# A two-layer image kernel: a gate's loads and the y stores issued in the middle of a tick instead of at its end

## The chip, the cores and the metric

The kernel runs on one core of a Trainium2 chip. The metric is the device time of one execution in microseconds; lower is better. Everything is float32.

## The reference

Input and output are `x` of shape 8 x 8 x 512 x 512 (batch elements, channels, rows, columns). Two residual layers follow each other, each on a group-normed input:

```python
x = x + L0(gn(x))        # spectral: a few Fourier modes of every channel, mixed and sent back
x = x + L1(gn(x))        # below

def L1(x):
    grid = x
    for _ in range(15):                               # coupled map: 15 steps per channel
        mapped = 3.9 * grid * (1 - grid)
        grid = 0.85 * (0.7 * mapped + 0.3 * conv3x3(mapped, K_local)) + 0.15 * x
    cml = clip(grid, 1e-4, 1 - 1e-4)
    nca = sigmoid(conv1x1(relu(conv3x3(x, Wp)), Wu))  # 128 hidden channels
    gin = concat([x, cml, nca])
    g = sigmoid(conv1x1(relu(conv3x3(gin, Wg1)), Wg2))
    return g * cml + (1 - g) * nca
```

## The kernel before

Four kinds of work are woven together by hand, and the order of the source is kept on every engine and queue (`keep_order`).

- *Steps.* The coupled map of an element lies in SBUF in sets of slabs: a first phase of four sets (channels 0 to 3) and a second of four sets and a tail. One step of one set is 96 matmuls (`Slabs.convolve`, L535), a `max` and add on DVE (L548), a square on ACT (L554), and an exchange of edge rows by DMA (`renew`: L581 and L582 on POOL's queue, L591 on SP's; the tail's on L648, L652 and L657). When a set has made its 15 steps, `leave` clips it and puts off its stores to the plane `cml` in HBM (L611) by one tick.
- *Rounds.* `Hidden.round` makes the 3x3 convolution to 128 hidden channels for four rows at a time (L734) from `cols`, which `load` (L717) brings in; `point` (L761) makes the 1x1 convolution after it. Every fourth round a tile `y` is full; ACT makes its sigmoid (L773), and its `store` to the plane `nca` (L776) is put off by one tick. `e.rows` counts the rows of `nca` that are stored.
- *Gates.* A gate is 12 rows of the final formula, 43 of them for each element. `load` takes two tiles from the shared slots: `gin` (three loads at L796, 1,024 KB together: input of the 3x3 convolution) and `mix` (three at L801, 576 KB: the rows that are mixed). `conv` (L811) gives `gin` back, `point` (L828, L832, L834) follows, and `finish` (L839) and the store to `out` (L846) are made after the first step of the next tick, and give `mix` back. The gates of an element are made while the next element takes its steps; the last element's gates are left for the end.
- *Spectral layer.* The next element's 16 channel tiles `x` come in (L183), go through layer 0 and are stored to the plane `xn` (L424).

A *tick* (`work`) is three steps, then `transfers()`, up to three rounds, and the matmuls of gates, hidden point and spectral pieces. `transfers()` issues the x loads and the loads of the next phase (`dE`, `dO`, L506). The gates' loads come last, with `others.load(gates)`, and then `tick()` advances the clock `now` and issues everything that was put off until then. There are 45 ticks for each element, and a final *drain* without steps for the last element's gates, in which `others.lag` is 2 and the y stores are issued from POOL's queue instead of SP's. Where `gates` is 2 in a tick with steps, one gate is loaded after the first step.

SBUF has 19 slots of 8 KB per partition. `shared.most` is 4, 7 or 3 of them, by the place in the element (`SHARED`, `MORE`, `LEAST`), for gates and the next element's `x`; of these `kept` are held back for `x`. Free slots are handed out in the order in which they came free, so a load into one may have to wait for the last reader of what lay there.

Of the kernel before, what the change touches and what calls it, by code (L numbers as in the profile page):

```python
# [41 lines left out]
P = 128  # L42
C = 8
N = 512
# [68 lines left out]
def view(t, offset, dims):  # L113

    return bass.AP(tensor=t.tensor, offset=t.offset + offset, ap=[list(d) for d in dims])
# [3 lines left out]
def conv_layers(ctx: ExitStack, tc: tile.TileContext, a, out):  # L119
# [10 lines left out]
    class Slots:  # L130
# [4 lines left out]
        def __init__(self, most):  # L135
            self.most, self.held = most, {}
# [15 lines left out]
    sets, shared = Slots(SLOTS), Slots(SHARED)  # L152
# [7 lines left out]
    pairs = [pp.tile([P, 2, N], F32, name=f"pair{i}") for i in range(4)]  # L160


    put_off, now = [], [0]

    def later(ticks, work):
        put_off.append((now[0] + ticks, work))
# [8 lines left out]
    def load(name, shape):  # L175
        t = cp.tile(shape, F32, name=name)
        nc.scalar.dma_start(out=t, in_=a[name])
        return t
# [8 lines left out]


    dft_y = load("dft_y", [P, 2, 32])
    dft_x = load("dft_x", [P, 2, 2, 8])  # L190
    waves = load("waves", [16, 5])
# [475 lines left out]
    class Phase:  # L667
# [23 lines left out]
        def squares(self, n):  # L691
            while self.squared < len(self.sets) and sets.room():
                if not self.ready(self.squared, 0, n + TICK):
                    break
                self.sets[self.squared].square()
                self.squared += 1
# [9 lines left out]
    class Hidden:  # L706
# [50 lines left out]
        def point(self, hs, ps):  # L757

            for r, h in hs:
                for g in range(4):  # L760
                    nc.tensor.matmul(  # L761
                        ps[32 * g : 32 * g + 32], w_u[:, r % 4], h[:, g],
                        start=(r == hs[0][0]), stop=(r == hs[-1][0]),
                        tile_position=(0, 32 * g),
                    )
            if hs[0][0] % 4 == 0:
                self.y = wk.tile([P, N], F32, tag="y", name="y", bufs=2)
                nc.scalar.copy(self.y, ps)  # L768
            else:
                nc.vector.tensor_tensor(self.y, self.y, ps, ALU.add)  # L770
            if r % 4 == 3:
                y, r0 = self.y, 4 * (r - 3)
                nc.scalar.activation(y, y, AF.Sigmoid, bias=b_u)  # L773

                def store():
                    (nc.gpsimd if others.lag else nc.sync).dma_start(  # L776
                        out=view(self.e.nca, (1 + r0) * C * N, [[N, P], [1, N]]), in_=y
                    )
                    self.e.rows = r0 + 16

                later(1, store)

    class Gate:

# [4 lines left out]
        def load(self):  # L789

            r0, self.at = self.r0, now[0]
            self.gin = shared.take([P, 4, N], "gin")
            self.mix = shared.take([P, 4, N], "mix")
            for q, src in enumerate((self.e.xn, self.e.cml, self.e.nca)):
                at, rows = (0, 48, 88)[q], (6, 5, 5)[q]
                nc.sync.dma_start(  # L796
                    out=self.gin[at : at + rows * C],
                    in_=view(src, r0 * C * N, [[N, rows * C], [3 * C * N, 4], [1, N]]),
                )
            for q, src in enumerate((self.e.xn, self.e.cml, self.e.nca)):  # L800
                nc.sync.dma_start(  # L801
                    out=self.mix[: GR * C, q],
                    in_=view(src, (r0 + 1) * C * N, [[N, GR * C], [1, N]]),
                )

        def conv(self, ps):

            gin, (x1, d, ng) = self.gin, (self.mix[: GR * C, q] for q in range(3))
            for n, (dx, lo, hi, at) in enumerate(SHIFTS):
                for j in range(4):  # L810
                    nc.tensor.matmul(  # L811
                        ps[32 * j : 32 * j + 32, lo:hi], gband[:, dx], gin[:, j, at : at + hi - lo],
                        start=(n == 0), stop=(n == 2), tile_position=(0, 32 * j),
                    )

            nc.gpsimd.tensor_tensor(d, d, ng, ALU.subtract)  # L816
            nc.vector.scalar_tensor_tensor(  # L817
                x1, x1, self.e.back[: GR * C, 1:2], ng, ALU.mult, ALU.add
            )
            shared.drop(gin)  # L820
            nc.vector.tensor_scalar(self.mix[:, 3], ps, b_g1, 0.0, ALU.add, ALU.max)  # L821
# [92 lines left out]
    class Others:  # L914


        def __init__(self):
            self.before, self.after, self.hold, self.limit = None, None, 0, 0
            self.mapped, self.lag = deque(), 0
            self.loaded, self.convolved, self.pointed = deque(), deque(), deque()  # L920

        def load(self, limit):
            if self.mapped and not (self.before and self.busy()):
                self.before = self.mapped.popleft()
            e, after = self.before, self.after
            kept = max(0, after.most() - len(after.x)) if after and after.pieces else 0
            for _ in range(limit):
                if not (e and e.gates) or shared.room() - kept < 2:
                    break
                if e.rows < min(e.gates[0].r0 + GR + 1, N) or len(e.mapped) <= 2 * SETS:  # L930
                    break
                g = e.gates.popleft()
                g.load()
                self.loaded.append(g)

        def busy(self):
            return self.before.gates or self.loaded or self.convolved or self.pointed

        def finish(self):
            while self.pointed:  # L940
                self.pointed.popleft().finish()

        def conv(self, ps):
            if not self.loaded or now[0] < self.hold or self.loaded[0].at + self.lag > now[0]:
                return False
            g = self.loaded.popleft()
            g.conv(ps)
            self.convolved.append((g, ps))
            return True
# [42 lines left out]
    def element(b):  # L992
        e = Element(b)
        phase(e.halves[0])
        phase(e.halves[1] + [e.tail])
        elements.append(e)
        return e

    e = element(0)
# [3 lines left out]
    others = Others()  # L1003
    for n in count():
# [5 lines left out]
        ps = next(turns)  # L1010
# [15 lines left out]
    def work(steps, rounds, e, after, gates, transfers, squares=lambda: None):  # L1026

        def half():
            used[0] += 1
            return halves[used[0] % 2]  # L1030

        settled = iter(())
        for n, (s, step) in enumerate(steps):
            ps = half()
            s.convolve(step, ps)
            next(settled, None)
            settled = s.settle(step, ps)
            next(settled)
            others.finish()
            if gates == 2:  # L1040
                others.load(1)
                gates = 1
        others.finish()
        transfers()
        for _ in range(rounds):
            e.hidden.round(half(), after, settled)
        next(settled, None)
        squares()


        first, second = halves[used[0] % 2], halves[(used[0] + 1) % 2]
        if not others.spectral(WIDE, second):
            used[0] += 1
            first, second = second, first
        groups = e.hidden.sums()
        if len(groups) == 2:
            e.hidden.point(groups.pop(0), first[1][:, 0])
        others.conv(first[0][:, 0])
        others.spectral(EARLY, [second[0][:, 0]])
        two = others.conv(second[0][:, 0])  # L1060
        if groups:
            e.hidden.point(groups[0], first[1][:, 1])
        others.spectral(FILL, [None])
        others.spectral(LATE, [second[1][:, 0], second[0][:, 0]])
        others.point()
        used[0] += two
        others.load(gates)
        tick()
        squares()

    def turn(at, rounds, e, after, gates):


        now_phases = [p for p in phases if at < p.end + TICK]

        def transfers():
            if others.after:
                others.after.fetch()
            for p in now_phases:
                p.fetch(at)  # L1080

        def squares():
            for p in now_phases:
                p.squares(at)

        for p in now_phases:
            p.prepare(at)
        steps = [slots[i] for i in range(at, at + TICK) if 0 <= i < len(slots)]
        work(steps, rounds, e, after and after.hidden, gates, transfers, squares)
# [4 lines left out]
    for b in range(B):  # L1094
        e = elements[b]
# [3 lines left out]
        first, second = phases[2 * b : 2 * b + 2]  # L1099
# [14 lines left out]
        for t in range(ticks):  # L1114
# [8 lines left out]
            gates = open_[t] + (left > sum(open_[t:]) and not (after and after.pieces))  # L1123
# [68 lines left out]
```

## Time and profile before

| | us |
|---|---|
| median of 3 runs | 9339.16 |
| lowest and highest | 9327.55, 9340.95 |
| the profiled execution | 9328.59 |
| its span, first to last instruction | 9326.8 |
| PE busy | 8776.0 |
| DVE, ACT, POOL busy | 5685.6, 4101.0, 3378.9 |
| mean granted clock of PE | 0.987 |

A row of a group in the profile names the line of the kernel, the engine and the operation, what is written and read (buffer numbers left out), how many there were, the busy time and the mean of one in ns; after the second bar stands the engine's idle time just before these instructions, and what ended most of it. "issue" means that no other engine and no transfer in the profile ended the wait. A row of waits gives total us, times and longest. SPq is SP's DMA queue. A row of the timeline gives the start, the time taken, and the instructions of one kind that follow each other. A row of a table of windows has the stretch, its length, the busy time of PE, PEld, DVE, ACT and POOL with counts, the granted clock of PE, the busy share of the DMA engines and the GB/s they moved.

### The profile page before, as it was taken

How to read it: one execution, taken by the hardware profiler on the slowest of the kernel's cores; microseconds unless marked ns; L12 is line 12 of the kernel's file. 1: busy time of each engine (PE TensorE's matmuls, PEld its weight loads, DVE VectorE, ACT ScalarE, POOL GpSimd, SP SyncE). 2: the span in 40 equal slices, each digit the busy share in tenths (PEclk: the TensorE clock that was granted, in tenths of full speed). 3: DMA queues.
4: the chain of work that ended last, by engine and by line, in shares of the span. 5: the costliest groups of instructions: out<-in, count | busy, mean ns of one | idle time of the engine just before them, and what ended most of it. 6: DMA issues, size and time to landing. Idle time of an engine off the chain costs nothing. (4 is left out here: it accounts for less than half of the span.)

```text
span 9326.8 us, 334742 instructions
## 1 busy us (share of the span) xinstructions
PE 8776.0 (94%) x150992; PEld 4165.1 (45%) x150992; DVE 5685.6 (61%) x5844; ACT 4101.0 (44%) x4285; POOL 3378.9 (36%) x4441
## 2 busy tenths in 40 slices
PE   5999999999999999999999999999999999899988
PEld 2445544444444444444444444444444444344433
DVE  5665567556665567655676556755567555555655
ACT  2445444444444444444444444444444444344422
POOL 3242334334343243433334343343433324453422
PEclk9999999999999999999999999999999999999999
DMA  5241356745566455754657546575455755665487
GB/s 158 79 127 39 96 150 167 171 109 152 148 178 146 112 155 145 184 137 112 169 146 176 129 108 167 156 179 126 111 158 167 173 117 129 144 153 119 105 212 184
DMA packets 697414, 1327.26 MB, mean 142 GB/s; under 512 B 146939, under 2 KB 152443, under 8 KB 668499
## 3 DMA queue, kind: packets, MB, share of 16 engines
q1 hardware_dynamic: 591840, 1244.38, 51.8%
q0 software_dynamic: 101792, 60.33, 3.0%
q8 instruction: 1187, 19.45, 0.9%
q14 instruction: 241, 1.97, 0.1%
q10 hardware_dynamic: 2354, 1.14, 0.0%
HBM read 977.48 MB, written 270.61 MB: 134 GB/s over the span
## 5 line engine op out<-in xcount | busy, mean ns | idle before, releaser
L535 PE MATMUL pair<-m,band 32*32 32x512 f32 x103680 | 3669.8, 605 | 205.2 <-issue 132.7
L554 ACT ACTIVATE m<-m 128x1024 f32<-128x1024 f32 x2016 | 2128.8, 1056 | 2081.0 <-DVE m L548 1994.9
L535 PEld LDWEIGHTS pair<-m,band 32*32 32x32 f32 x103680 | 2166.3, 103 | 1664.5 <-issue 820.3
L734 PE MATMUL pair<-cols,w_p 32*128 32x511 f32 (+1 forms) x24576 | 2800.1, 596 | 64.3 <-DMA cols<-xn 36.0
L734 PEld LDWEIGHTS pair<-cols,w_p 32*128 32x128 f32 x24576 | 1311.0, 185 | 1565.4 <-issue 1189.8
L548 DVE SCALAR_TENSOR_TENSOR m<-pair,dO 128x1024 f32<-128x1024 f32 x1152 | 1356.9, 1219 | 1040.0 <-PE pair L535 772.5
L581 POOL DMA_DIRECT2D m<-m x1568 | 855.3, 545 | 3061.0 <-ACT m L554 2983.1
L742 DVE TENSOR_SCALAR h<-pair,b_p 128x1024 f32<-128x1024 f32 x1024 | 1311.9, 1283 | 1045.4 <-PE pair L734 1035.3
L548 DVE SCALAR_TENSOR_TENSOR m<-pair,dE 128x1024 f32<-128x1024 f32 x1008 | 1187.3, 1219 | 867.3 <-PE pair L535 635.3
L740 ACT ACTIVATE h<-pair,b_p 128x1024 f32<-128x1024 f32 x1024 | 1141.2, 1115 | 1206.6 <-PE pair L734 1196.6
L834 POOL TENSOR_TENSOR mix<-mix 96x512 f32<-96x512 f32 x344 | 451.0, 1317 | 2010.8 <-ACT mix L832 1958.3
L761 PE MATMUL pair<-h,w_u 128*32 128x512 f32 x8192 | 999.0, 597 | 56.9 <-DVE y L770 30.4
L811 PE MATMUL pair<-gin,w_g 128*32 128x511 f32 (+1 forms) x8256 | 963.2, 604 | 64.5 <-DMA gin<-nca 45.8
L582 POOL DMA_DIRECT2D m<-m x1568 | 840.5, 536 | 36.7 <-issue 30.7
L811 PEld LDWEIGHTS pair<-gin,w_g 128*32 128x32 f32 x8256 | 254.3, 111 | 721.2 <-issue 654.8
L761 PEld LDWEIGHTS pair<-h,w_u 128*32 128x32 f32 x8192 | 246.2, 110 | 674.6 <-issue 516.5
L816 POOL TENSOR_TENSOR mix<-mix 96x512 f32<-96x512 f32 x344 | 446.4, 1300 | 191.0 <-DMA mix<-nca 143.5
L773 ACT ACTIVATE y<-y,b_u 128x512 f32<-128x512 f32 x256 | 184.9, 722 | 748.2 <-DVE y L770 747.9
L768 ACT COPY y<-pair 128x512 f32<-128x512 f32 x256 | 149.9, 586 | 693.3 <-PE pair L761 686.0
L558 POOL TENSOR_SCALAR dO<-dO 128x2048 f32<-128x2048 f32 x72 | 398.1, 5529 | 88.1 <-DVE m L548 87.0
L817 DVE SCALAR_TENSOR_TENSOR mix<-mix,back 96x512 f32<-96x512 f32 x344 | 379.7, 1104 | 81.0 <-DMA mix<-nca 63.9
L821 DVE TENSOR_SCALAR mix<-pair,b_g 128x512 f32<-128x512 f32 x344 | 257.2, 748 | 248.2 <-PE pair L811 238.2
(91 smaller groups left out, 3023.6 us busy)
## 6 DMA issues: line engine op xcount, KB each, us to landing
gin<-xn SPq DMA_DIRECT2D x344, 384.0 KB
cols<-xn SPq DMA_DIRECT2D x256, 512.0 KB
x<-in_x SPq DMA_DIRECT2D x120, 1024.0 KB
gin<-cml SPq DMA_DIRECT2D x344, 320.0 KB
gin<-nca SPq DMA_DIRECT2D x344, 320.0 KB
dE<-xn SPq DMA_DIRECT2D x288, 256.0 KB
dO<-xn SPq DMA_DIRECT2D x288, 256.0 KB
mix<-xn SPq DMA_DIRECT2D x344, 192.0 KB
```

The source lines that it names most:

```text
L535: nc.tensor.matmul(ps[h // 2][32 * t : 32 * t + 32, h % 2], band[at, self.channel(step - 1, h, t), dx], m[at, t, dx : dx + N], start=(n == ...
L548: nc.vector.scalar_tensor_tensor(u[:, at], ps[q], FLOOR, d[:, at], ALU.max, ALU.add)
L554: nc.scalar.square(u[:, at], u[:, at])
L581: nc.gpsimd.dma_start(out=view(tb, rb, dims), in_=view(ta, ra, dims))
L582: nc.gpsimd.dma_start(out=view(ta, ra + s, dims), in_=view(tb, rb + s, dims))
L734: nc.tensor.matmul(ps[g // 2][:, g % 2, lo:hi], w_p[p, dx, i % 2], self.cols[p, i // 2, at : at + hi - lo], start=(n == 0), stop=(n == 2), ...
L740: nc.scalar.activation(h[:, :2], ps[0], AF.Relu, bias=b_p)
L742: nc.vector.tensor_scalar(h[:, 2:], ps[1], b_p, 0.0, ALU.add, ALU.max)
L761: nc.tensor.matmul(ps[32 * g : 32 * g + 32], w_u[:, r % 4], h[:, g], start=(r == hs[0][0]), stop=(r == hs[-1][0]), tile_position=(0, 32 * g),)
L811: nc.tensor.matmul(ps[32 * j : 32 * j + 32, lo:hi], gband[:, dx], gin[:, j, at : at + hi - lo], start=(n == 0), stop=(n == 2), tile_positi ...
L816: nc.gpsimd.tensor_tensor(d, d, ng, ALU.subtract)
L834: nc.gpsimd.tensor_tensor(d, d, mix[: GR * C, 2], ALU.mult)
```

## The change

Three things change, all of them in the order in which work is issued.

1. `Gate.load` is split: `load` takes and loads `gin`, `load_rows` takes and loads `mix`.
2. After `transfers()`, ahead of the rounds, a tick with steps calls `others.load(gates, early=True)`. Where two shared slots are free beyond those kept, a gate is loaded whole there. Where one is free, and a gate that is already loaded waits for its convolution, only `load_rows` is issued, and the gate goes to `begun`; its `gin` is then loaded at the end of the tick, by the call that was there before. What was loaded early is taken off that call's number. `conv` keeps a gate from being convolved in the tick that loads it, except for the second convolution of a tick with two gates (`double`).
3. The store of `y` is put into `rows_due`, and issued at the head of the next tick's `transfers()`, instead of in `tick()` at the end of its own tick.

```diff
-                later(1, store)
+                rows_due.append(store)
...
             self.gin = shared.take([P, 4, N], "gin")
-            self.mix = shared.take([P, 4, N], "mix")
             for q, src in enumerate((self.e.xn, self.e.cml, self.e.nca)):
...
+        def load_rows(self):
+
+            r0 = self.r0
+            self.mix = shared.take([P, 4, N], "mix")
             for q, src in enumerate((self.e.xn, self.e.cml, self.e.nca)):
...
-        def load(self, limit):
+            self.begun = deque()
+
+        def load(self, limit, early=False):
...
+            while self.begun and not early:
+                if shared.room() - kept < 1:
+                    return
+                g = self.begun.popleft()
+                g.load()
+                self.loaded.append(g)
+                limit -= 1
             for _ in range(limit):
-                if not (e and e.gates) or shared.room() - kept < 2:
+                room = shared.room() - kept
+                if not (e and e.gates) or room < 1 or room < 2 and not (early and self.loaded):
                     break
...
                 g = e.gates.popleft()
+                if room < 2:
+                    g.load_rows()
+                    self.begun.append(g)
+                    break
                 g.load()
+                g.load_rows()
                 self.loaded.append(g)
...
-        def conv(self, ps):
-            if not self.loaded or now[0] < self.hold or self.loaded[0].at + self.lag > now[0]:
+        def conv(self, ps, soon=False):
+            if not self.loaded or now[0] < self.hold:
+                return False
+            if self.loaded[0].at + (self.lag if soon else max(self.lag, 1)) > now[0]:
                 return False
...
+        double = gates == 2 and not others.lag
...
         others.finish()
         transfers()
+        if steps:
+            had = len(others.loaded) + len(others.begun)
+            others.load(gates, early=True)
+            gates -= len(others.loaded) + len(others.begun) - had
         for _ in range(rounds):
...
-        two = others.conv(second[0][:, 0])
+        two = others.conv(second[0][:, 0], double)
...
         def transfers():
+            while rows_due:
+                rows_due.pop()()
             if others.after:
```

More of the change, by code (lines that the diff above doesn't have):

```diff
@@ L160, in conv_layers @@
     pairs = [pp.tile([P, 2, N], F32, name=f"pair{i}") for i in range(4)]
-    put_off, now = [], [0]
+    put_off, now, rows_due = [], [0], []
     def later(ticks, work):
@@ L932, in load @@
                 g = e.gates.popleft()
+                if room < 2:
+                    g.load_rows()
+                    self.begun.append(g)
+                    break
                 g.load()
+                g.load_rows()
                 self.loaded.append(g)
         def busy(self):
-            return self.before.gates or self.loaded or self.convolved or self.pointed
+            ahead = self.loaded or self.begun
+            return self.before.gates or ahead or self.convolved or self.pointed
         def finish(self):
```

## The prediction

> **What bounds the kernel now.** First the page's busy times and its groups, for the engine that sets the end and what it waits for.
>
> ```profile
> PE 8776.0 (94%) x150992; PEld 4165.1 (45%) x150992; DVE 5685.6 (61%) x5844; ACT 4101.0 (44%) x4285; POOL 3378.9 (36%) x4441
> ...
> q1 hardware_dynamic: 591840, 1244.38, 51.8%
> ...
> q8 instruction: 1187, 19.45, 0.9%
> ...
> L535 PE MATMUL pair<-m,band 32*32 32x512 f32 x103680 | 3669.8, 605 | 205.2 <-issue 132.7
> ```
>
> PE is busy 94% of the span and no other engine reaches two thirds of it, so the tick is PE's and only what makes PE idle or slow can be won. The largest idle time stands before L535, the step matmuls, and its releaser is "issue": neither data nor another engine. In the waits of PE the rows that concern gates are small:
>
> ```profile
> PE pair L535 <- issue: 132.7, 83, 4.5
> PE pair L811 <- DMA gin<-nca: 45.8, 15, 5.8
> ```
>
> Next I read PE's timeline tick by tick. A tick has three steps (288 step matmuls), up to three rounds, then a gate's matmuls. Two ticks of one element:
>
> ```profile
> 4171.69 4.53 PE L535 MATMUL pair<-m,band 32*32 32x512 f32 x130
> 4177.89 5.49 PE L535 MATMUL pair<-m,band 32*32 32x512 f32 x158 [1.67 <-issue]
> 4183.31 8.00 PE L734 MATMUL pair<-cols,w_p 32*128 32x512 f32 x72
> ...
> 4197.38 9.75 PE L535 MATMUL pair<-m,band 32*32 32x512 f32 x288
> ```
>
> Undisturbed, the 288 take 9.75 us; in the first tick they stop in the middle of a step. I took (last end minus first start) of the 288 in each of the 360 ticks from that listing: the excess over 9.75 sums to 324 us, and 287 of it stands in 81 ticks. The windows say what those have in common:
>
> ```profile
> 4197.40:4207.10 9.70, 9.70 (x295) 6.13 (x292) 5.37 (x5) 5.15 (x6) 3.31 (x5) 1.00 0.67 170
> 3904.00:3920.70 16.70, 12.23 (x295) 5.90 (x292) 5.36 (x5) 7.63 (x8) 13.38 (x17) 0.80 0.96 217
> 3920.70:3934.80 14.10, 14.10 (x135) 5.82 (x132) 7.62 (x7) 5.45 (x6) 5.83 (x8) 1.00 0.87 245
> ```
>
> Columns end with the granted clock, the DMA share and GB/s. At share 0.96 the steps took 16.7 us, 4.47 of them idle to "issue", at clock 0.80. At 0.87 the rounds after them (14.1 us) had PE busy throughout. So a loaded DMA hurts the steps and not the rounds. The cause I read: queue q8 is PE's instruction stream (150,992 matmuls and as many weight loads, at 64 bytes, are 19.33 of its 19.45 MB), in blocks of 16.4 KB, 256 instructions. The steps use a block in 4.35 us (9.75 x 128/288), the rounds in some 14 (8.00 x 128/72). Counting blocks against the trace's DMA packets, a block's fetch begins about when the block before it begins to run; under 130 GB/s it is never late in the steps, from 180 to 230 GB/s about one in six is, and in the rounds none is at any load.
>
> What loads the DMA during steps is the seam of the ticks. SP's timeline there:
>
> ```profile
> 4191.40 0.39 SPq L717 DMA_DIRECT2D cols<-xn  x1
> 4191.84 0.46 SPq L796 DMA_DIRECT2D gin<-xn  x1
> ...
> 4194.47 0.42 SPq L801 DMA_DIRECT2D mix<-nca  x1
> 4198.13 0.34 SPq L776 DMA_DIRECT2D nca<-y  x1
> 4203.88 0.84 SPq L846 DMA_DIRECT2D out<-mix  x1
> ```
>
> One gate is 1,600 KB (gin 384+320+320, mix 3 x 192), y 256 KB: issued 6 us before the steps and just inside them, some 8 us of transfer, half under the steps.
>
> **The Trainium skill.** "Runtime: NRT & Kernel Launch", section "Instruction fetch mechanics": instructions come by DMA in 16 KiB blocks of 256, fetched while the current one runs; the block size agrees with q8, but "mostly hidden" does not hold here. "DMA: Bandwidth & Descriptors", section "Issuing engines are not separate DMA queues": all queues share 16 engines and interleave; the late fetches beside q1's traffic agree. "Perfetto Trace Analysis", section "The 4-stage abstract model": instructions are 64 bytes, used above; 19.33 of 19.45 MB agrees.
>
> **The change part by part.** No instruction is added or removed: 344 gates of six loads, 256 y stores; no tick more or fewer, since each tick still loads as many gates as its shared slots allow. What changes is SP's order. The room in the middle of each tick follows from the slot limits (7, 4 or 3, less what the next element's x tiles keep); I counted it through the listing.
>
> *Whole gates.* In 160 ticks with one gate two slots are free in the middle, and all six loads move from the end to ahead of the rounds. SP then reaches them right after the out store, 6.5 us into the tick (4203.88 above); gin can go at once, mix waits for that store to land. 1,856 KB with y at some 220 GB/s is 8.5 us: done before the next steps. What then stands behind mix's wait on SP is the third step's past store (read by the tail's next step, more than 9.75 us on) and the cols load, which waits on PE anyway and is used a tick later: no cost. Of the steps that follow these ticks in elements 2 to 7, 120 (without two heavier places in each) have 44.8 us of excess. Steps with under 750 KB moved beside them average 0.12 us (19.6 us in 157 ticks), so 14 stay: **-30**. In the last element ticks are 17 us and the seam is tighter: 28 such steps, 29.9 us; I leave 8: **-22**. The tick after the xn stores begin the next phase: 9.8 us in six, half goes: **-5**. The third tick of an element has 34 us, but there 2 MB of x sits in a queue already moving 245 GB/s; reordering it wins nothing: **0**, from -15 to 0.
>
> *Rows only.* In 67 ticks one slot is free: mix moves to the middle, gin stays at the end, and takes the slot that this tick's gate conv frees, so it now waits for L811. Before, gin went beside cols and mix waited:
>
> ```profile
> SPq L801 <- PE pair L811: 137.2, 38, 11.5
> SPq L776 <- ACT y L773: 587.7, 157, 12.8
> ```
>
> So 1,024 KB, not 576 + 256, is issued last. Behind it stand the xn and cml stores; the gate itself is wanted 20 us later. 192 KB more beside the steps, at the 0.15 us between my classes of 500 and 750 to 1,000 KB, is 10; relief earlier takes a little: **+8**, bounded by -20 and +90 (below).
>
> *y stores.* The second wait above goes: y is long done by the middle of the next tick. Rows become visible there, ahead of the gate test, so no gate comes later. Alone, 256 KB out of about 70 more seams: **-4**, 0 to -10.
>
> *Double gates.* In 37 ticks one gate goes after the first step and is convolved in the same tick. The new conv test keeps this; the L811 waits (7 ticks of the last element, 3.4 to 7.4 us, 33 together) stay: **0**, -10 to +10.
>
> *The drain.* It has no steps, so no early loads. But the last y ahead of it now goes to POOL's queue, not behind 12 cml stores on SP, where it was issued at 8849.43, 10 us after its ACT operation, and occupied SP 7.7 us; ACT waited 6.8 us for its buffer. Of PE's following 16.5 us wait for cols some goes too: **-7**, from 0 to -20. POOL has nothing queued there.
>
> Sum: -30 - 22 - 5 + 8 - 4 - 7 = **-60 us**. The profiled execution took 9328.59 us (span 9326.8), 10.6 below the median of 9339.16; the difference is applied to the median: **9279**.
>
> **Rivals.** (1) *The loads arrive where they did.* SP is in order: L846 waits for the finish of the gate (2298.6 us in all), L591 for ACT (1116.0), and mix for the out store. If these hold the loads until the rounds end, nothing moves but y: 9335. Against: L846 was through at 6.5 us into the tick above, and the third step's past store now comes behind the loads. (2) *Slower: gin behind the conv.* If in the 67 rows-only ticks the next steps go from the class of 1,000 to 1,250 KB (0.45 us) to that of 1,500 to 2,000 KB (1.79), that is 67 x 1.34 = +90, and with -60 - 8 for the rest it ends at 9361. It decides from 1 us per such tick up. Against: mix and y leave the same place, 832 of 1,024 KB. (3) *More than forecast.* If the saturated ticks gain as well (rows-only steps have 109 us of excess, the third ticks 34), a third of that is -48: about 9230.
>
> **How the numbers follow.** Forecast 0.55, larger gain 0.22, nothing moves 0.11, slower 0.12. A measurement of this kernel tells about 0.2% (19 us) from no change. Faster than that: forecast and larger gain, 0.78; same 0.11; slower 0.11. The range runs from the larger gain with the drain's full 20 (9215) to the first rival (9335).
>
> **What would show it.** Right: L535's "issue" idle falls from 132.7 to about 90; in the ticks of an element's last third SP's L796 stands ahead of L717 and L776 ahead of both; the wait of L776 on ACT y nearly gone; busy times and counts as before. Wrong: the same "issue" idle with loads moved (then the fetch is not held by this traffic); new idle before L811 from gin (the rows-only order is late); or a longer L734 (the loads do harm the rounds).

## The result and the profile after

| | before | after |
|---|---|---|
| median, us (5 runs each) | 9333.21 | 9283.59 |
| lowest to highest | 9319.23 to 9340.95 | 9279.62 to 9291.93 |
| span of the profiled execution | 9326.8 | 9277.7 |

The ratio is 0.9947, with a 95% interval of 0.9936 to 0.9958: faster by 0.5%, against a forecast of 0.6%. On a second chip the changed kernel gave 0.9946 (0.9932 to 0.996); one of its six runs there was slow (10237.06 us, at a mean granted clock of 0.84) and enters no ratio and no median here. Lines from 795 on have moved: the gate's gin loads are L795 after (L796 before), mix L805 (L801), the gate's conv L815 (L811), its point L832, L836 and L838 (L828, L832, L834), its finish L843 (L839) and the out store L850 (L846).

First the page of the changed kernel, for the same groups:

```profile
PE 8751.8 (94%) x150992; PEld 4174.8 (45%) x150992; DVE 5682.2 (61%) x5844; ACT 4101.6 (44%) x4285; POOL 3382.9 (36%) x4442
...
q8 instruction: 1187, 19.45, 0.9%
...
L535 PE MATMUL pair<-m,band 32*32 32x512 f32 x103680 | 3647.0, 603 | 183.8 <-issue 106.6
```

The same 150,992 matmuls and the same instruction stream; PE is busy 24 us less, and the idle time before the step matmuls fell from 205.2 to 183.8 us. Of that, "issue" fell from 132.7 to 106.6. Part of a starved step is thus booked as busy time (matmuls that follow each other more slowly, some at half the clock), which is why the length of the 288 matmuls is the better measure: over the 360 ticks its excess over 9.75 us went from 323.8 to 279.9 us. That is 44 of the 49 us between the spans.

Part of these 44 us is a matter of the granted clock: the steps ran at half clock for 138.9 us before and for 101.4 us after, which makes 19 us if half of that time is lost (an estimate). Most of these stretches begin at the stops and are not a cause apart. Of the 50 at half clock in the trace before, 36 begin close to a restart of PE after more than 0.5 us of idle time (from 0.5 us ahead of it to 2 us behind it), where 7% would by chance; of the 43 after the change it is 29.

What the change did to a tick is seen in PE's timeline, here in the tick that lost 1.67 us before and the one after it:

```profile
4168.18 9.75 PE L535 MATMUL pair<-m,band 32*32 32x512 f32 x288
4177.86 8.00 PE L734 MATMUL pair<-cols,w_p 32*128 32x512 f32 x72
...
4191.93 9.75 PE L535 MATMUL pair<-m,band 32*32 32x512 f32 x288
```

Both now take 9.75 us. SP's timeline in the first of them:

```profile
4174.69 0.83 SPq L850 DMA_DIRECT2D out<-mix  x1
4175.62 0.46 SPq L776 DMA_DIRECT2D nca<-y  x1
4176.17 0.38 SPq L795 DMA_DIRECT2D gin<-xn  x1
...
4179.59 0.42 SPq L805 DMA_DIRECT2D mix<-nca  x1
4185.94 0.39 SPq L717 DMA_DIRECT2D cols<-xn  x1
```

The y store and the six loads stand right behind the out store, from 7.4 us after the tick's start (4168.18), and ahead of the cols load. Before, the loads came after cols and y last of all. The windows of the steps of the first tick and of what follows them, before (first two rows) and after (next two), and of the overfull tick whose steps the prediction showed at 217 GB/s:

```profile
4171.70:4183.20 11.50, 9.83 (x291) 5.18 (x288) 5.37 (x5) 4.39 (x5) 2.38 (x3) 1.00 0.30 81
4183.20:4197.30 14.10, 14.10 (x136) 5.47 (x126) 8.25 (x8) 5.86 (x6) 5.28 (x9) 1.00 0.38 85
4168.20:4177.90 9.70, 9.70 (x295) 6.14 (x292) 5.36 (x5) 4.55 (x5) 2.38 (x3) 1.00 0.18 48
4177.90:4191.90 14.00, 14.00 (x128) 5.45 (x126) 8.30 (x8) 5.71 (x6) 5.29 (x9) 1.00 0.66 172
3899.40:3913.00 13.60, 10.01 (x295) 5.30 (x292) 5.37 (x5) 7.64 (x8) 11.59 (x14) 1.00 1.01 228
```

Columns end with clock, DMA share and GB/s. The transfers of this quiet tick (one in which little but a gate, y and cols is on its way) have left the steps (81 GB/s before, 48 after) for the rounds (85 before, 172 after), where PE is busy for all of the 14.00 us. The mean rate of a window does not decide by itself: the steps at 81 GB/s lost 1.9 us, while those at 170 GB/s in the prediction's table lost nothing. What counts is what is on its way when a block of instructions is fetched. The overfull tick is still overfull: share 1.01 in its steps, which take 13.6 us, after 16.7 before.

The waits of PE and of SP that the forecast spoke of:

```profile
PE pair L535 <- issue: 106.6, 76, 4.2
...
PE pair L815 <- DMA gin<-nca: 36.2, 13, 6.6
```

```profile
SPq L795 <- PE pair L815: 201.4, 37, 11.1
...
SPq L805 <- DMA out<-mix: 61.0, 77, 2.8
...
SPq L776 <- ACT y L773: 45.2, 8, 13.0
```

Columns are total us, times, longest. y's wait for ACT fell from 587.7 us to 45.2; gin's wait for the gate's conv, the price of the case of one free slot, rose from 81.5 to 201.4 us; mix's wait for the out store is 0.8 us a time. None of the three is PE's time.

### The profile page after: what moved, and what is told of

Same layout as the page of the kernel before. It is cut to its first block, busy times and chain, and to the rows that moved or that the text cites. A ratio compares the mean times of both kernels' runs of the same rounds, so it can differ in the third digit from the quotient of the medians.

```text
span 9277.7 us, 334691 instructions
## 1 busy us (share of the span) xinstructions
PE 8751.8 (94%) x150992; PEld 4174.8 (45%) x150992; DVE 5682.2 (61%) x5844; ACT 4101.6 (44%) x4285; POOL 3382.9 (36%) x4442
## 5 line engine op out<-in xcount | busy, mean ns | idle before, releaser
L535 PE MATMUL pair<-m,band 32*32 32x512 f32 x103680 | 3647.0, 603 | 183.8 <-issue 106.6
L838 POOL TENSOR_TENSOR mix<-mix 96x512 f32<-96x512 f32 x344 | 451.9, 1319 | 2009.1 <-ACT mix L836 1945.4
L815 PE MATMUL pair<-gin,w_g 128*32 128x511 f32 (+1 forms) x8256 | 960.5, 602 | 59.9 <-DMA gin<-nca 36.2
L815 PEld LDWEIGHTS pair<-gin,w_g 128*32 128x32 f32 x8256 | 253.8, 111 | 715.6 <-issue 645.6
L820 POOL TENSOR_TENSOR mix<-mix 96x512 f32<-96x512 f32 x344 | 448.1, 1305 | 152.6 <-DMA mix<-nca 93.1
L558 POOL TENSOR_SCALAR dO<-dO 128x2048 f32<-128x2048 f32 x72 | 397.5, 5521 | 88.2 <-DVE m L548 87.0
L821 DVE SCALAR_TENSOR_TENSOR mix<-mix,back 96x512 f32<-96x512 f32 x344 | 360.2, 1047 | 73.1 <-DMA mix<-nca 60.1
```

Of the source, the lines that this page charges most:

```text
L535: nc.tensor.matmul(ps[h // 2][32 * t : 32 * t + 32, h % 2], band[at, self.channel(step - 1, h, t), dx], m[at, t, dx : dx + N], start=(n == ...
L815: nc.tensor.matmul(ps[32 * j : 32 * j + 32, lo:hi], gband[:, dx], gin[:, j, at : at + hi - lo], start=(n == 0), stop=(n == 2), tile_positi ...
L838: nc.gpsimd.tensor_tensor(d, d, mix[: GR * C, 2], ALU.mult)
```

## The experiments

Two theories were tried first. Mine: PE's steps starve for their own instructions when large transfers run beside them, so *where* in the tick the transfers run is what counts. The first rival: SP was held by y's wait, and everything behind it came late.

**The y stores alone.**

```diff
 # the kernel before, and only:
-                later(1, store)
+                rows_due.append(store)
...
         def transfers():
+            while rows_due:
+                rows_due.pop()()
```

> The kernel before with the y stores alone moved to the middle of the next tick; the gates' loads stay at the end. Theory (PE's steps wait for their own instructions when large transfers run beside them): 256 KB leaves about two seams in three, so the gain is small, 0 to -10 us on 9333, and the excess of the steps (324 us before, 280 with the whole change) stays above 310. Rival (SP was held by waiting for ACT's y, 588 us in all, and everything behind it came late): most of the gain of 50 us is here already, 9290 to 9300.

Measured: 1.0004 (0.9997 to 1.0011), no gain. The step excess is 331 us. In the 78 ticks 29 to 41 of elements 2 to 7 (ticks counted from 0, elements from 1; all follow a tick with a whole gate) it fell from 38.0 to 25.2 us, but in the last element's ticks with a single gate it rose from 29.9 to 47.6. y is not what the gain rests on.

**The gates' loads alone.**

```diff
 # the changed kernel, and only:
-                rows_due.append(store)
+                later(1, store)
```

> The changed kernel with the y stores put back to the end of their tick. Theory: 9285 to 9300, nearly the whole gain, with a step excess of 280 to 295 us, and y's wait for ACT back in SP's waits. Rival (SP held by y): 9320 or more.

Measured: 0.9934 (0.992 to 0.9947), so all of the gain and perhaps a little more. Step excess 262 us, less than the 280 of the whole change. Both lie below what was expected (9285 to 9300 us, 280 to 295 us of excess; measured 9265.76 and 262): the loads alone do more than I gave them. SP's wait for y is longer than in the kernel before (587.7 us):

```profile
SPq L776 <- ACT y L773: 852.7, 162, 13.0
```

More waiting at y than in the kernel before, and a faster kernel: the rival falls. That moving y costs something is suggested and not shown, since the intervals overlap.

**No case of one free slot.**

```diff
-                if not (e and e.gates) or room < 1 or room < 2 and not (early and self.loaded):
+                if not (e and e.gates) or room < 2:
                     break
```

> The changed kernel without the case of one free slot: there mix and gin both stay at the end of the tick. Theory: in these 67 ticks mix leaves the seam but gin comes later to it, so they nearly cancel: 9280 to 9295, within 8 us of the changed kernel. Rival of the prediction (gin behind the gate's conv costs over 1 us a tick): 9220 to 9265. If mix's leaving is what counts there (rows-only steps lost 12 us of excess): 9290 to 9300.

Measured: 0.9959 (0.9947 to 0.9971). The interval overlaps that of the whole change. In the profiles the 66 such ticks of elements 2 to 7 show a trade: with the case, the steps after them have 88.2 us of excess and the rest of these ticks takes 1028.0 us; without it, 95.5 and 1020.7. The sums agree within 0.1 us. Moving mix alone relieved the steps by 7 us and gave it back in the same ticks. The prediction's slower rival (90 us from gin behind the conv) is excluded.

**The cause by itself: a copy that touches no SBUF.** Into 78 quiet ticks of the changed kernel I put a 1 MB copy from HBM to HBM, once at the end and once ahead of the rounds. Both are issued from ACT's queue.

```diff
+    def copy():
+        if copied[0]:                      # ticks 28 to 40 of elements 2 to 7
+            nc.scalar.dma_start(out=spare[0], in_=x[0, 0])
...
+        copy()                             # e7: ahead of the rounds
         for _ in range(rounds):
...
         others.point()
+        copy()                             # e6: at the end of the tick
```

> The changed kernel plus one copy of 1 MB from HBM to HBM (it touches no SBUF), issued from ACT's queue at the very end of 78 ticks (ticks 29 to 41 of elements 2 to 7), so that it runs under the next steps. It computes nothing. Theory (the steps starve for instructions when the DMA engines are loaded): the 78 steps behind it go from some 0.1 us of excess each to 0.7 or more, +40 to +120 us on the changed kernel, as idle of L535 before issue. Rival (the steps lose to transfers that write SBUF while PE reads it): within 10 us of the changed kernel.

> The same 78 copies, issued from the same queue ahead of the rounds of the same ticks. Theory: within 10 us of the changed kernel, since the rounds use their instructions more slowly than a loaded fetch brings them. Rival (what counts is how much is moved in a tick, not where): the same loss as with the copies at the end.

Measured, beside the changed kernel run again on that chip (0.9946):

> The changed kernel once more, as the base of the three runs beside it. 0.994 to 0.996 of the kernel before.

| | ratio to the kernel before | 95% | excess of the 78 steps behind the copies, us |
|---|---|---|---|
| changed kernel again | 0.9946 | 0.9932 to 0.996 | 4.3 |
| copies at the end | 0.9988 | 0.9982 to 0.9994 | 41.0 |
| copies ahead of the rounds | 0.9946 | 0.9933 to 0.9959 | 2.9 |

(The kernel before has 38.0 us in the same 78 steps.) The same bytes from the same queue cost 0.0042 of 9327, about 39 us, at the end of the tick, and nothing some 13 us earlier. (The 39 us lie just under the 40 to 120 expected: the 78 steps have 0.5 us of excess each and not 0.7, since only 36 of them lost more than 0.3 us.) The clock is not the reason: in these 78 steps PE ran at half clock for 2.0 us with the copies at the end and for 1.4 us with the copies ahead of the rounds. PE's timeline in one of the ticks with the copy at the end (its lines are five higher, so the step matmul is L540):

```profile
4239.30 6.58 PE L540 MATMUL pair<-m,band 32*32 32x512 f32 x193
4246.64 3.39 PE L540 MATMUL pair<-m,band 32*32 32x512 f32 x95 [0.76 <-issue]
```

and with the copy ahead of the rounds:

```profile
4216.37 9.75 PE L540 MATMUL pair<-m,band 32*32 32x512 f32 x288
```

With the copy at the end the stop falls inside a step, after 193 matmuls, where nothing but the next instructions is missing: "issue" again. The windows of these steps and of the rounds that the earlier copy ran beside:

```profile
4239.30:4250.00 10.70, 9.94 (x295) 5.42 (x292) 5.37 (x5) 4.92 (x5) 3.81 (x6) 1.00 0.53 158
4226.10:4237.10 11.00, 10.78 (x96) 3.83 (x94) 8.13 (x7) 5.90 (x7) 5.68 (x9) 1.00 0.97 261
```

The steps lost 1 us beside 158 GB/s; in the rounds PE was busy for 10.78 of 11.00 us beside 261 GB/s. Since the copy neither reads nor writes SBUF, a clash of transfers with PE's reads of SBUF is not needed for the loss. That the amount moved in a tick decides, and not its place, is excluded.

**The first gate two ticks later.** The prediction's third tick of an element (tick 3, counted from 0) was not helped by the change (33.9 us of excess in six of them before, 42.3 after): two x tiles, a gate and cols are on their way at once there.

```diff
-GATES_FROM, SPECTRAL_FROM = 1, 0
+GATES_FROM, SPECTRAL_FROM = 3, 0
```

> The changed kernel with the first gate of an element allowed two ticks later (GATES_FROM 3 for 1), out of the ticks in which the next element's first x tiles come in. Theory: the third tick's steps (42 us of excess in six of them) lose a part of their 1.6 MB of backlog: -10 to -30 us. Rival (the x tiles alone keep the transfers full there): within 8 us; the two gates are made up for in further double ticks, at no cost in matmuls.

Measured: 0.9925 (0.9911 to 0.9938), 21 us below the changed kernel beside it (9262.72 to 9283.83), and the third tick's excess is 18.8 us: 23.5 us of the 42.3 went, where the gate's 1.6 MB were taken out.

```profile
PE pair L535 <- issue: 84.3, 69, 4.9
```

**The xn stores to the middle as well.**

```diff
-                later(1, store)
+                xn_due.append(store) if e.b else later(1, store)
...
+        while xn_due:                      # ahead of the rounds
+            xn_due.pop(0)()
```

> The changed kernel with the xn stores (2 MB after every second x tile pair, so far at the end of a tick) also moved to just ahead of the rounds of the next tick; the x slots come free that much later. Theory: the steps of the ticks behind these stores (excess some 9 us per element over four ticks) are relieved: -20 to -45 us on the changed kernel, 9240 to 9265. Rival (the middle of the tick is already full of x loads, so the transfers reach into the next steps anyway, or x arrives late): 9280 or slower.

Measured: 0.9924 (0.9911 to 0.9937). The eight ticks 11 to 18 of an element, where these 2 MB stores fall, go from 48.3 to 24.5 us of excess over six elements. But the step excess as a whole is 287 us, not less than the changed kernel's 280. The profiled run was the slowest of the five (9275.33 us, where the median is 9254.62), so the trace hardly shows the gain. The ratio lies below the changed kernel's 0.9947, with an interval that touches its own; how the gain splits is open.

**Both, and more of the same.** Four further runs joined these moves:

> The changed kernel with both moves that won: xn stores in the middle of the tick, and the first gate two ticks later. Theory: both relieve different steps, so they add up: 20 + 22 us below the changed kernel, 0.989 to 0.991 of the kernel before. Rival (they free the same transfers): 0.992 to 0.993.

> The same with the y stores back at the end of their tick. If moving y costs a little where the middle is full (the loads alone gave 0.9934 against 0.9947 of the whole change, intervals that touch): 5 to 12 us below the run beside it with y moved. If y is neutral: within 5 us of it.

> As the first of this group, and the cml stores (12 of up to 240 KB when a set has left) moved to the middle of the next tick as well. Theory: the steps of ticks 19 to 22 and of an element's first tick lose 3 MB at their start, -10 to -40 us on that run. Rival (the middle of these ticks is full of the next phase's loads, 2 MB each, so the transfers only change places): within 8 us, or slower.

> As the first of this group, with the first gate four ticks later instead of two. Theory: the third tick is already relieved by two, so -5 to +5 us. If the four further double ticks, each with loads after a step that PE must wait for, cost: +5 to +15 us.

| | ratio | 95% |
|---|---|---|
| xn stores mid, gates 2 ticks later | 0.9929 | 0.9917 to 0.9941 |
| the same, y at the end | 0.9923 | 0.991 to 0.9935 |
| the first with cml stores mid | 0.995 | 0.9938 to 0.9962 |
| the first with gates 4 ticks later | 0.9942 | 0.9929 to 0.9954 |

They do not add up. The 78 steps have 16.6 us of excess in the first of the four, where they have 4.3 in the changed kernel, 3.1 with the gates later alone and 8.0 with the xn stores in the middle alone; why the two together disturb ticks that each leaves quiet is not shown. With the cml stores in the middle as well the gain is given back, 22 us on the first of the four. Of that the five ticks from 18 to 22 show 7 us of excess (89.1 to 95.8), and all steps together 5 (284.4 to 289.5), so the expected cause, a middle full of the next phase's loads, explains a part at most. The best five (this table's first two, the gates later, xn mid, the loads alone: 0.9923 to 0.9934) can't be told apart. All five lie below the changed kernel's 0.9947, with intervals that overlap or barely clear it.

## Why the prediction was right, point by point

The sign, the size and the mechanism held. That 9283.59 came so near to 9279 is in part luck: 60 us of gain were forecast and 50 measured, and the forecast started from 9339.16, the median of three runs, where that of five is 9333.21. The terms of the sum, from the profiled executions before and after, and from the changed kernel's second profile, on the other chip, against the same trace of before:

| step of the prediction | forecast, us | measured, us | second profile, us |
|---|---|---|---|
| whole gates, elements 2 to 7, 120 ticks | -30 | -35.2 (44.7 to 9.5) | -33.0 |
| whole gates, last element, 28 ticks | -22 | -8.7 (29.9 to 21.2) | -8.4 |
| tick 18 | -5 | +2.1 | +1.3 |
| third tick | 0 | +8.4 (33.9 to 42.3) | +10.6 |
| rows only: steps, then the rest of these ticks | +8 | -12.2 + 9.3 | -15.9 + 14.5 |
| y alone | -4 | +4 in its own run (-3 to +10) | |
| double gates: the steps behind them | 0 | -1.4 | -1.3 |
| drain | -7 | -1.7 | 0.0 |

The two profiles of one kernel differ by up to some 5 us in a term, so the small rows say little. The rows from the traces sum to -39 and -32 us, where the spans fell by 49 and 45: 10 and 13 us went elsewhere, above all in what follows the steps, in ticks of two gates (-8 and -5) and in other ticks (-6 and -3). The forecast had nothing there, and the cause is open. So misses of both signs cancel in the sum.

**Whole gates.** The step is the forecast's heart and was a little too careful: 0.08 us stays in a tick, not 0.12. The loads make the larger part of it: with them alone the 120 steps have 10.6 us of excess, with y alone 31.7.

**The last element** is the term that was mis-sized. Its two ticks 40 and 41 show why: tick 40 went from 5.05 to 0.31 us of excess, and the next from 0.36 to 9.99. In the changed kernel's PE timeline:

```profile
8715.03 3.40 PE L535 MATMUL pair<-m,band 32*32 32x512 f32 x96
8725.91 8.85 PE L535 MATMUL pair<-m,band 32*32 32x512 f32 x192 [7.48 <-ACT mix L836]
```

and in POOL's:

```profile
8716.50 5.38 POOL L558 TENSOR_SCALAR dO<-dO 128x2048 f32<-128x2048 f32 x1
...
8723.87 1.27 POOL L820 TENSOR_TENSOR mix<-mix 96x512 f32<-96x512 f32 x1
```

PE's second step needs the bank that ACT's L836 reads, which waits for POOL's L820, which stands behind the third of POOL's 5.4 us operations at L558. While tick 40 starved, POOL had time for them: in both kernels it reaches L820 (L816 before) 27.6 us after the start of tick 40. The faster PE meets POOL instead: the gain is given back as a new wait, and from the start of tick 40 to that of tick 42 it is 45.75 us before and 45.82 after. The same 7.48 us stood there when the changed kernel was run again. The other 26 single-gate ticks of the last element gave up 14 us and keep 10.9, which is more than the 8 that I left for all 28.

**Third tick and tick 18.** I had 0 and -5, from -15 to 0 for the first. The third tick became slower than my bound allowed, and the traces say which part of the change did it: it has 43.6 us of excess with the y stores alone moved, 36.3 with the loads alone, and from 42.2 to 45.4 in every trace with y moved and the first gate where it was. So the moved y stores cost the third tick some 8 us; I had y as a small gain everywhere. Why they cost there is not shown. The run with the first gate later shows the gate's bytes to be the cause of over half of the tick's excess.

**Rows only.** The term's sign was wrong (+8; steps and rest together -3 and -1), within its bounds.

**The drain.** The y store did go to POOL's queue (19 instead of 18), and ACT's wait of 6.8 us for its buffer is gone. But SP's place was taken at once by the first gin load, which needed 7.76 us to be accepted behind the 12 cml stores; cols came no earlier, and PE's wait for it is 18.1 us where it was 16.5. The 7.67 us that y had taken to be accepted were thus the queue's and not y's own.

**The rivals.** Loads that stay where they were: refuted by SP's timeline. Gin behind the conv: refuted by the run without that case. Saturated ticks gaining as well: they did not by this change, though two further moves of the same kind win some of that.

**What the Trainium skill said.** "Runtime: NRT & Kernel Launch", section "Instruction fetch mechanics", describes the fetch of the next 256 instructions while the current ones run. Its "mostly hidden" holds for the rounds, where 14 us pass for a block, and not for the steps, where 4.33 us do (9.75 x 128/288; the prediction's 4.35 is a slip). That the stops are late fetches can be read from the DMA packets of the trace: before the change PE stops for more than 0.3 us inside a run of step matmuls 100 times, and 79 of these stops end 1.1 to 1.8 us after an instruction packet of q8 has landed, where 13% would by chance; after the change it is 72 of 90. That the instruction queue is delayed beside other transfers is these traces' finding.

The prediction's shares were too favourable. I counted the blocks of the steps again, with the rate over the 2 us from the start of the block before, and a block as late when PE stopped at its start for more than 0.3 us behind its packet. Below 130 GB/s 1 of 275 was late and not none; from 180 to 230 GB/s it was 16 of 66, one in four and not one in six; above that 36 of 83. With the change the blocks at 180 GB/s and above, the ones at risk, fell from 149 to 105. The rounds are not wholly free either: PE lost 4.1 us to "issue" in them before, 1.43 of it three matmuls behind a step.

"Issue" at 106.6 us missed the 90 that I had named as a sign. It stays in the ticks that the change left full.

## What to carry to other kernels

When an engine that never waits for data has gaps before "issue" in the middle of a run of equal instructions, compare its instruction rate and the DMA load at that moment. Dense stretches of small matmuls are the place to keep clear of large transfers, and slow stretches the place to put them, at no cost in bytes. And size a gain by ticks of one kind: where the queue is already full, reordering moves the loss about, and where another engine was covered by the stall, it comes up as the next wait.

## What the runs showed of the hardware

I had not expected how small a load is enough. One 1 MB copy beside a 9.75 us stretch of 576 PE instructions costs 0.5 us of it on the mean (36.7 us over 78), and beside a stretch of the same kernel with a third of that rate it costs nothing. The stop falls where a block of instructions ends, and PE goes on 1.1 to 1.8 us after the packet has landed, in 79 of 100 stops. So its place looks arbitrary in the source: after 130 matmuls in a tick of the kernel before and after 193 in one with the copies. And a stop often brings half clock after it, so that it costs more than its idle time: 36 of the 50 stretches at half clock begin at a restart of PE.
